# A graph layer on one core: in the first part of group 0, VectorE normalises the tile two batches ahead behind conv1's additions in place of ahead of them

## The chip, the core and the metric

The kernel runs on one core of one Trainium2 chip. The metric is the device time of one execution in microseconds (us); lower is better. A core has five engines that run beside each other, each with a queue of its own: TensorE (PE in the profile; PEld is its loading of weights), VectorE (DVE), ScalarE (ACT), GpSimd (POOL) and SyncE (SP), which here only issues DMAs. Matmuls write to PSUM, of which the kernel uses eight banks; VectorE and ScalarE carry the results from there to SBUF, and so make a bank free for the next matmul.

## What is computed

There are 32 batches of 512 tokens with 256 channels. For each batch (shortened from the reference; the batch norms are constants here and so scale and shift):

```
h   = relu(layernorm(x))                              # over the channels
c   = relu(bn1(conv1(h)))                             # a 256x256 matrix for each token
c   = relu(bn2(conv2(c)) + h)                         # 17 taps along the tokens
s   = h @ w_se.T + b_se                               # three numbers for each token
A   = exp(-|s_n - s_m|^2) * adj
nmp = A @ relu(h @ w_msg.T + b_msg)
r, z, n from a GRU cell with input [c, nmp], state h
out = x + (1 - z) * n + z * h
```

All of it is in 32-bit floats. Conv2 is done by windows of 64 tokens and a transform along the tokens: conv1's result is transformed (`windows_to_freq`), multiplied there with the transformed taps, and transformed back later. The transform of the 17 taps themselves (`weights_to_freq`) is done in the kernel as well, in pieces that are strewn in between the batches of the part that this change touches.

## The kernel before

The 32 batches form two groups of 16 (`GB`). For each group a first part makes h, conv1 and the transform, and a second part (`nodes`) makes the products with the taps and the messages; at the end the gates run over pairs of batches. The change is in the first part of group 0, the branch `if g == 0` in `first_part`. That whole part is built under a manual schedule: every engine carries out its instructions in the order in which the code writes them.

One iteration of the loop for batch b from 2 on writes, in this order:

1. `load_x(b + 3)`: a DMA for the tile of x three batches ahead, on SyncE's queue for b under 3 and on GpSimd's from then on. There are three buffers for x.
2. `statistics(b + 2)`: VectorE's four `bn_stats` (line 392), four `bn_aggr` (394) and one addition (397), then a power on GpSimd that makes rstd (398). These are the means and the factors of the layer norm, two batches ahead.
3. `transpose_h(b + 1)`: TensorE transposes the normalised tile xn (line 419) in eight pieces into two banks, and VectorE takes the relu out of them into hT (423). HT is then written to memory (424) for later parts.
4. `slot()`: for b over 2, a piece of the taps' transform: four matmuls into four banks (line 363; each has two records), and four copies into wst, on ScalarE (373) or VectorE (371). For b = 2 this piece stands ahead of the statistics.
5. `normalise(b + 2)`: four VectorE instructions (line 411) that make xn of the tile two batches ahead from x, the mean and rstd. There are two buffers for xn.
6. `conv1(b)`: 16 matmuls (line 439) from hT of this batch into two banks, eight to each; for each bank an addition of a row on VectorE (442) and a relu on ScalarE (443). The result is h1.
7. `slot()`: a second piece of the taps' transform. Behind every second batch the load of further taps hangs on it, on GpSimd's queue; the finished wst tiles are written to memory from SyncE's queue (377).
8. `windows_to_freq(b - 1)`: the transform of the conv1 result of the batch before: 16 matmuls in two passes of eight records each (line 454) into four banks, and four ScalarE copies into xf (457).
9. `slot()`: a third piece, for b = 12 and b = 14 alone.

All banks come from one pool of eight and are handed out in turn. A plain iteration takes 16 of them (two for the transposes, four for a piece of the taps, two for conv1, four for a piece, four for the windows), so each of these steps finds the same banks in each round, and a step's first matmul waits until the copy or addition that read this bank eight banks ago is done. Conv1 of batch b reads hT that was made one iteration earlier; the transposes of batch b + 1 read xn that was made one iteration earlier.

The order within an iteration of the loop is thus the order in VectorE's queue: statistics, two hT, the copies of the first piece, four normalise, two additions, the copies of the second piece.

Of the kernel before, what the change touches and what calls it, by code (L numbers as in the profile page):

```python
# [162 lines left out]
def gnn_layer(  # L163
# [38 lines left out]
    def bank(name):  # L202
        return psum.tile([P, N], FP, tag="bank", name=name)
# [9 lines left out]
    def load_x(b, queue=nc.sync):  # L213
        X[b] = pools["ahead" if b == GB else "first"].tile([P, NC, D], FP, tag="x", name=f"x_{b}", bufs=1 if b == GB else 3)
        queue.dma_start(X[b], x[b].rearrange("(c p) d -> p c d", p=P))
# [46 lines left out]
    def batch_norm(k, scale, shift, engine):  # L262
        engine.tensor_scalar(scale, at[k + "_v"], BN_EPS, None, op0=ALU.add)
        nc.gpsimd.tensor_tensor(scale, scale, minus_half[:, :DC], op=ALU.pow)
        engine.tensor_mul(scale, scale, at[k + "_g"])
        engine.tensor_mul(shift, at[k + "_m"], scale)
        engine.tensor_sub(shift, at[k + "_b"], shift)
# [11 lines left out]
    def bn1_row(i, v, ones, diags):  # L279
        for c in range(DC):  # L280
            diag = diags[:, i, c, :]
            nc.scalar.activation(diag, ident, AF.Copy, scale=v[:, c : c + 1])
            nc.tensor.matmul(row1[i][:, c * P : (c + 1) * P], ones, diag, start=True, stop=True)
# [6 lines left out]
    def scale_w1():  # L290
        t = W2P.pop("w1")
        for c in range(DC):
            nc.vector.tensor_mul(w1[:, c, :].rearrange("p (i q) -> p i q", i=DC), by_parity(t[:, c, :]),
                                 by_parity(row1[0][:, :D]))
# [93 lines left out]
    def statistics(b):  # L388
        stats = work.tile([P, NC, 6], FP, tag="stats", name=f"stats_{b}")
        mv = work.tile([P, NC, 2], FP, tag="mv", name=f"mv_{b}")  # L390
        for c in range(NC):
            nc.vector.bn_stats(stats[:, c, :], X[b][:, c, :])
        for c in range(NC):
            nc.vector.bn_aggr(mv[:, c, :], stats[:, c, :])
        rstd = work.tile([P, NC], FP, tag="rstd", name=f"rstd_{b}")
        STATS[b] = mv, rstd
        nc.vector.tensor_scalar(rstd, mv[:, :, 1], LN_EPS, None, op0=ALU.add)
        nc.gpsimd.tensor_tensor(rstd, rstd, minus_half[:, :NC], op=ALU.pow)

    def normalise(b, by_scalar=()):  # L400
        mv, rstd = STATS.pop(b)
        XN[b] = pools["first"].tile([P, NC, D], FP, tag="xn", name=f"xn_{b}", bufs=2)
        if by_scalar:
            shift = work.tile([P, NC], FP, tag="shift", name=f"shift_{b}")
            nc.vector.scalar_tensor_tensor(shift, mv[:, :, 0], -1.0, rstd, op0=ALU.mult, op1=ALU.mult)
        for c in range(NC):
            dst, src = by_half(XN[b][:, c, :]), halves(X[b][:, c, :])
            if c in by_scalar:
                nc.scalar.activation(dst, src, AF.Identity, bias=shift[:, c : c + 1], scale=rstd[:, c : c + 1])
            else:  # L410
                nc.vector.tensor_scalar(dst, src, mv[:, c, 0:1], rstd[:, c : c + 1], op0=ALU.subtract, op1=ALU.mult)
        del X[b]
# [14 lines left out]
    def place_h1(b):  # L427
        H1[b] = pools["first"].tile([P, NC, D], FP, tag=f"h1{b % 2}", name=f"h1_{b}", bufs=1)

    def conv1(b):  # L430
        if b not in H1:
            place_h1(b)
        h = N // D
        for c0 in range(0, NC, h):
            p = bank(f"pc1_{b}_{c0}").rearrange("p (c d) -> p c d", d=D)
            for j in range(h):
                c = c0 + j
                for ic in range(DC):
                    nc.tensor.matmul(p[:, j, :], HT[b][:, ic, c * P : (c + 1) * P], w1[:, ic, :],  # L439
                                     start=(ic == 0), stop=(ic == DC - 1))  # L440
            h1 = H1[b][:, c0 : c0 + h, :]
            nc.vector.tensor_add(h1, p, shift1_row[:, None, :].to_broadcast([P, h, D]))
            nc.scalar.activation(h1, h1, AF.Relu)
        if b % GB < GB - 2:
            del HT[b]
# [721 lines left out]
    def first_part(g, freq, between, left=()):  # L1167


        b0, b1 = g * GB, (g + 1) * GB  # L1170
        for b in range(b0, b0 + 3):
            if b not in X and (g == 0 or b == b0):
                load_x(b)
        if g == 0:
            t = XN[b0] = pools["first"].tile([P, NC, D], FP, tag="xn", name="rows", bufs=2)
            ones, diags = t[:, 0, :P], t[:, 1:3, :].rearrange("p i (c m) -> p i c m", m=P)
            nc.vector.memset(ones, 1.0)

            for _ in range(10):
                nc.tensor.matmul(row1[1][:, :P], ident, fr.rearrange("p g c k -> p (g c k)"), start=True, stop=True)  # L1180
            batch_norm("bn1", scale1, shift1, nc.gpsimd)
            bn1_row(0, scale1, ones, diags)
            bn1_row(1, shift1, ones, diags)
        if b0 not in STATS:
            statistics(b0)
        normalise(b0, range(2, NC) if g == 0 else ())
        if g == 0:
            scale_w1()
            shift_w1()
        left = list(left)  # L1190

        def fill():
            for step in left.pop(0) if left else ():
                step()

        if g > 0:
            place_h1(b0)
            load_x(b0 + 1)
            fill()
            load_x(b0 + 2)  # L1200
        transpose_h(b0)
        statistics(b0 + 1)
        fill()
        normalise(b0 + 1, range(NC) if g > 0 else ())
        if g > 0:
            statistics(b0 + 2)
        fill()
        for b in range(b0, b1):
            if b + 3 < b1:
                load_x(b + 3, nc.sync if b < 3 else nc.gpsimd)  # L1210
            if b == b0:
                conv1(b)
                one, two = between(0) if g == 0 else ([], [])
                for step in one:
                    step()
                fill()
                if g == 0:
                    transpose_h(b + 1)
                    statistics(b + 2)
                    normalise(b + 2)  # L1220
                else:
                    normalise(b + 2)
                    transpose_h(b + 1)
                fill()
                xf, last_two = freq(g), two
                continue
            if g == 0:

                slots = last_two if b == b0 + 1 else between(b - b0)

                def slot():
                    for step in slots.pop(0) if slots else ():
                        step()

                if b == b0 + 1:
                    between(b - b0)
                    conv1(b)
                    slot()
                if b == b0 + 2:
                    slot()  # L1240
                if b == b1 - 1:
                    by_chunks(b - 1)
                    load_h(b0)
                if b + 2 < b1:
                    statistics(b + 2)
                if b + 1 < b1:
                    transpose_h(b + 1)
                if b > b0 + 2:
                    slot()
                if b + 2 < b1:  # L1250
                    normalise(b + 2)
                if b > b0 + 1:
                    conv1(b)
                    slot()
                if b == b1 - 1:
                    by_chunks(b)
                windows_to_freq(b - 1, xf)
                slot()
                continue
            if b == b1 - 1:  # L1260
                by_chunks(b - 1)
                load_h(b0)
            if b + 2 < b1:
                statistics(b + 2)
            if b + 1 < b1:
                transpose_h(b + 1)
            if b + 2 < b1:
                normalise(b + 2)
            one, two = between(b - b0)
            conv1(b)  # L1270
            for step in one:
                step()
            windows_to_freq(b - 1, xf)
            for step in two:
                step()
        if g > 0:
            by_chunks(b1 - 1)
        windows_to_freq(b1 - 1, xf)
        return xf
# [273 lines left out]
```

## Time and profile before

| | us |
|---|---|
| median of three runs | 1731.29 (1730.93 to 1731.61) |
| the profiled execution | 1731.29 |
| its span, first to last instruction | 1729.5 |
| TensorE busy in the span | 1714.3 |
| VectorE busy in the span | 1299.3 |
| from conv1 of batch 2 to conv1 of batch 15 | 120.35 |
| of these, TensorE busy | 119.77 |
| of these, VectorE busy | 95.62 |

Busy times are the union of what the profile records for an engine. The ends of matmuls are modelled there, so a stretch in which the engine is busy throughout may still hold waits. The profile gives for each instruction its start and, in brackets, how long its engine sat idle before it and which event ended that idle time. The chain of waits follows the work that ended last back to the start: at each step to what released the instruction, or to the one before it on its engine. In the names, L439 is line 439 of the kernel, and out<-in says what the instruction writes and reads.

Over the stretch from batch 2 to batch 15, the longest waits in total are ScalarE's relu for VectorE's addition (43.0 us, 22 times) and GpSimd's power for VectorE's part of rstd (37.7 us, 7 times). VectorE waited 6.9 us for conv1's matmuls (10 times), 4.3 us for tiles of x (4 times) and once 1.8 us for rstd. TensorE's transposes waited for ScalarE's copies twice, 0.6 us in all.

### The profile page before, as it was taken

The page shows a single profiled execution, that of the slowest core. Times are in us where ns is not written, and L with a number is a line of the kernel's source. Part 1 is how long each engine was busy: PE and PEld are TensorE (multiplying, and loading weights), DVE is VectorE, ACT ScalarE, POOL GpSimd, SP SyncE. Part 2 cuts the span into 40 slices and gives each one's busy share as a digit, 9 for nine tenths or more (in the row PEclk, how much of TensorE's full clock was granted, in tenths as well). Part 3 has the DMA queues.
Part 4 walks back from the last instruction along what each step waited for, and adds up shares of the span by engine and source line. Part 5 has one row for each costly group of instructions (what it writes and reads, how often), then busy time and mean ns, then how long its engine had stood idle before and what let it go on. Part 6 is the DMA issues. An engine that isn't in the chain of part 4 may idle for free.

```text
span 1729.5 us, 24317 instructions
## 1 busy us (share of the span) xinstructions
PE 1714.3 (99%) x7920; PEld 1319.8 (76%) x7920; DVE 1299.3 (75%) x2599; ACT 692.1 (40%) x1669; POOL 1086.6 (63%) x1074
## 2 busy tenths in 40 slices
PE   8999999999999999999999999999999999999998
PEld 6777888888998888887877778777877787778744
DVE  7876877776996677676587778877887778777867
ACT  4556655553446555554322232232323232323221
POOL 3331788687655677777767657665667556755551
PEclk9999999999999999999999999999999999999999
DMA  9989987885778888888433454235523553345423
GB/s 250 304 283 263 262 237 242 252 231 183 269 246 232 268 246 238 234 254 309 115 106 71 79 128 119 69 69 128 128 67 70 120 128 91 75 91 128 110 55 73
DMA packets 311681, 295.07 MB, mean 171 GB/s; under 512 B 147436, under 2 KB 241164, under 8 KB 311172
## 3 DMA queue, kind: packets, MB, share of 16 engines
q1 hardware_dynamic: 301588, 265.17, 55.9%
q0 software_dynamic: 6960, 26.65, 4.8%
q10 hardware_dynamic: 3008, 1.72, 0.3%
q8 instruction: 63, 1.03, 0.2%
q14 instruction: 62, 0.51, 0.1%
HBM read 194.31 MB, written 99.16 MB: 170 GB/s over the span
## 4 chain that ended last, share of the span: by engine, by line
PE 93%; DVE 2%; DMA 2%; POOL 1%; SPq 1%; issue 1%; ACT 0%; POOLq 0%; DVEq 0%
PE pg L915 29%; PE pn L932 16%; PE py L503 11%; PE pn L670 10%; PE pm L558 6%; PE pc L439 6%; PE pc L878 3%; PE px L454 3%; PE pd L608 2%; PE pw L363 1%; PE phT L419 1%; PE pz L932 1%; PE pg L932 1%; PE pn L653 1%; PE pc L881 1%
## 5 line engine op out<-in xcount | busy, mean ns | idle before, releaser
L470 POOL TENSOR_TENSOR wsum<-wt 128x512 f32<-128x512 f32 x66 | 93.6, 1418 | 97.9 <-DMA wt<-wd 69.2
L503 PE MATMUL py<-wt,xf 128*128 128x256 f32 x640 | 154.2, 384 | 0.0
L915 PE MATMUL pg<-te,sw 128*128 128x256 f32 x600 | 154.0, 379 | 0.0
L906 ACT ACTIVATE rz<-rz,brz 128x256 f32<-128x256 f32 x180 | 86.3, 504 | 147.1 <-DVE rz L921 147.1
L503 PEld LDWEIGHTS py<-wt,xf 128*128 128x128 f32 x640 | 117.1, 190 | 34.9 <-issue 21.2
L915 PEld LDWEIGHTS pg<-te,sw 128*128 128x128 f32 x600 | 114.0, 190 | 15.5
L618 DVE TENSOR_TENSOR A<-A,at 128x512 f32<-128x512 f32 x124 | 118.5, 995 | 6.3 <-ACT A L614 2.8
L915 PE MATMUL pg<-tn,sw 128*128 128x256 f32 x480 | 123.2, 379 | 0.0
L915 PE MATMUL pg<-hn,sw 128*128 128x256 f32 x480 | 123.2, 379 | 0.0
L932 PE MATMUL pn<-tn,sw_n 128*128 128x512 f32 x256 | 120.3, 592 | 0.0
L1077 ACT ACTIVATE pn<-nt,vech 128x512 f32<-128x512 f32 x45 | 31.1, 692 | 219.1 <-DVE nt L1074 139.8
L439 PE MATMUL pc<-w,hT 128*128 128x256 f32 x512 | 117.7, 383 | 0.9 <-DVE hT L423 0.9
L558 PE MATMUL pm<-wmsg,hq 128*128 128x259 f32 x512 | 117.3, 381 | 0.0
L439 PEld LDWEIGHTS pc<-w,hT 128*128 128x128 f32 x512 | 94.6, 190 | 23.9 <-issue 6.4
L812 POOL TENSOR_TENSOR tn<-hn 128x512 f32<-128x512 f32 x64 | 86.2, 1367 | 35.6 <-PE pn L932 35.6
L558 PEld LDWEIGHTS pm<-wmsg,hq 128*128 128x128 f32 x512 | 96.5, 189 | 14.6
L915 PEld LDWEIGHTS pg<-hn,sw 128*128 128x128 f32 x480 | 91.1, 190 | 18.3 <-issue 3.4
L915 PEld LDWEIGHTS pg<-tn,sw 128*128 128x128 f32 x480 | 91.2, 190 | 12.4
L921 DVE TENSOR_TENSOR ct<-pg,ct 128x256 f32<-128x256 f32 x180 | 74.6, 415 | 33.0 <-PE pg L915 23.5
L932 PEld LDWEIGHTS pn<-tn,sw_n 128*128 128x128 f32 x256 | 48.6, 190 | 61.2 <-issue 50.9
L932 PE MATMUL pn<-hn,sw_n 128*128 128x512 f32 x192 | 90.5, 593 | 0.1
L915 PE MATMUL pg<-tec,sw 128*128 128x256 f32 x300 | 89.2, 379 | 0.0
(236 smaller groups left out, 4321.3 us busy)
## 6 DMA issues: line engine op xcount, KB each, us to landing
wt<-wd SPq DMA_DIRECT2D x80, 512.0 KB, 6.2
adj<-in_adj_dram SPq DMA_DIRECT2D x128, 256.0 KB, 5.8
wd<-wst SPq DMA_DIRECT2D x64, 320.0 KB, 5.4
yd<-y SPq DMA_DIRECT2D x76, 256.0 KB, 5.1
hd<-hT SPq DMA_DIRECT2D x32, 512.0 KB, 4.7
nd<-nmp SPq DMA_DIRECT2D x32, 512.0 KB, 3.0
xb<-in_x_dram SPq DMA_DIRECT2D x128, 128.0 KB, 6.3
out_dram<-xb SPq DMA_DIRECT2D x122, 128.0 KB, 2.8
```

The lines of the kernel that those rows point to most:

```text
L439: nc.tensor.matmul(p[:, j, :], HT[b][:, ic, c * P : (c + 1) * P], w1[:, ic, :], start=(ic == 0), stop=(ic == DC - 1))
L454: nc.tensor.matmul(p[:, j * 2 * L : (j + 1) * 2 * L], H1[b][:, c0 + j, ic * P : (ic + 1) * P], fwd, start=True, stop=True)
L470: nc.gpsimd.tensor_tensor(t, WT[g, u][:, 0], WT[g, u][:, 1], op=ALU.add)
L503: nc.tensor.matmul(dst, v[:, ic, :], w[:, ic, :], start=(ic == 0), stop=(ic == DC - 1))
L558: nc.tensor.matmul(p[:, : D + NS], hq[:, ic, c * P : (c + 1) * P], wmsg[:, ic, :], start=(ic == 0), stop=(ic == DC - 1))
L618: nc.vector.tensor_mul(A[b][:, mc, :], EXP.pop((b, mc)), AT.pop((b, mc)))
L670: nc.tensor.matmul(bk, left[:, k, :], right[:, k, :], start=(first and k == 0), stop=(k == 1), skip_group_check=True)
L812: nc.gpsimd.tensor_tensor(dst[:, k], x[:, k], y[:, k], op=op)
L906: nc.scalar.activation(at(dst), at(src), AF.Sigmoid, bias=brz[:, o : o + 1], scale=sign)
L915: nc.tensor.matmul(bk, SW["hk"][:, k, s, :], c if k == 2 else hn[:, k], start=(onto is None and k == 0), stop=(k == K3 - 1), skip_group_ch ...
L921: nc.vector.tensor_tensor(at(dst), at(x), at(y), op=op)
L932: nc.tensor.matmul(bk[:, t], weight(q, k, o), terms[k][q][:, t], start=(first and i == 0), stop=(i == len(ks) - 1), skip_group_check=True)
```

## The change

`normalise(b + 2)` is written behind `conv1(b)` instead of ahead of it. The conditions stay the same. It holds for b from 2 to 13; for b = 1, conv1 stands further up and nothing changes, and from b = 14 on there is no tile two batches ahead in this group.

```diff
                 if b > b0 + 2:
                     slot()
+                if b > b0 + 1:
+                    conv1(b)
                 if b + 2 < b1:
                     normalise(b + 2)
                 if b > b0 + 1:
-                    conv1(b)
                     slot()
```

Conv1's matmuls and relus are on TensorE and ScalarE, where the normalise has no instruction, so the order on these two engines is as before, and so is that of GpSimd and of the DMA queues. On VectorE the order becomes: statistics, two hT, the copies of the first piece, two additions, four normalise, the copies of the second piece.

## The prediction

> **What bounds the kernel now.** I read the page first, then the chain of waits in order of time over the first 220 us, then the timeline of the stage that the change touches, then the DMA share in windows of 2 us. From the page:
>
> ```profile
> PE 93%; DVE 2%; DMA 2%; POOL 1%; SPq 1%; issue 1%; ACT 0%; POOLq 0%; DVEq 0%
> ```
>
> TensorE carries the chain; VectorE holds 2% of it. So VectorE's order matters only where TensorE is kept waiting. TensorE's busy share cannot show where that is (10.00 of 10 us in most windows), since waits inside a stream of matmuls count as busy. I therefore took the pace of the loop: the times at which conv1's matmuls of batch b start (line 439). They are 27.57 for batch 2, then 37.47, 46.43, 55.39, 64.34, 74.63, 83.58, 92.54, 101.50, 110.93, 119.88, 130.02 (batch 13), 138.97, 147.92. The plain distance is 8.95 us. Longer ones are 2 to 3 (9.90), 6 to 7 (10.29), 10 to 11 (9.43), and 12 to 13 (10.14, of which 1.03 is a third piece of the kernel transform; 0.16 remains). The loss is 0.95 + 1.34 + 0.48 = 2.77 us. The plain iteration, of batch 4, in the timeline (start, duration, engine, idle time before it):
>
> ```profile
> 46.43 3.72 PE L439 MATMUL pc<-w,hT 128*128 128x256 f32 x16
> 47.77 1.37 DVE L411 TENSOR_SCALAR xn<-x,mv,rstd 128x256 f32<-128x256 f32 x4
> 49.05 0.68 DVE L442 TENSOR_TENSOR h<-pc,shift_row 128x512 f32<-128x512 f32 x1
> 50.08 1.10 PE L363 MATMUL pw<-w2p,taps 17*80 17x512 f32 x8
> 50.19 0.69 DVE L442 TENSOR_TENSOR h<-pc,shift_row 128x512 f32<-128x512 f32 x1 [0.46 <-PE pc L439]
> 51.11 2.44 PE L454 MATMUL px<-fwd,h 128*128 128x160 f32 x16
> 51.33 0.69 DVE L371 COPY wst<-pw 80x512 f32<-80x512 f32 x1 [0.45 <-PE pw L363]
> 53.39 1.04 PE L419 MATMUL phT<-ident,xn 128*128 128x128 f32 x8
> 54.03 1.29 DVE L423 TENSOR_SCALAR hT<-phT 128x512 f32<-128x512 f32 x2 [0.22 <-PE phT L419]
> 55.39 3.72 PE L439 MATMUL pc<-w,hT 128*128 128x256 f32 x16
> ```
>
> Here VectorE waits for TensorE three times and TensorE for nobody: TensorE sets the pace. Two of the three losses, in the chain of waits (start, duration, what):
>
> ```profile
> 31.41 1.05 DVE xn L411 x3
> 32.46 0.61 DVE h L442
> 33.09 1.23 ACT h L443 x2
> 34.32 0.48 ACT wst L373
> ...
> 34.85 1.14 PE phT L419 x8
> ...
> 67.24 0.97 POOL rstd L398
> 68.24 1.38 DVE xn L411 x4
> 69.62 0.61 DVE h L442
> 70.25 0.62 ACT h L443
> ...
> 71.38 0.57 ACT wst L373
> 72.00 1.14 PE phT L419 x8
> ```
>
> Both run the same way: normalise (xn), then conv1's addition (h), ScalarE's relu, ScalarE's copies out of the kernel-transform banks (wst), and only then may TensorE reuse these banks. The normalise stands at the head. In batch 6 it was itself held 1.77 us by GpSimd's rstd, which was late behind a load of vectors.
>
> **What the Trainium skill says.** "PSUM — Partial Sum Buffer", section "Engine vs sequencer instructions", has VectorE's and ScalarE's queues strictly first in, first out. The trace agrees: the additions of batch 6 started at 69.53, though their matmuls had ended by 67.99. "Perfetto Trace Analysis", "Optimizing Scalar/DVE Operations", says that part of a recorded duration overlaps the next instruction. It does: a normalise instruction is recorded at 402 ns, but four take 1.28 us from the first to the next addition. I count from start to start. The same page, "Identifying the Most-Contended Engine", calls matmul busy share a poor measure; the 10.29 us distance inside fully busy windows shows it.
>
> **The change part by part.** Nothing is added or removed: 12 times (batches 2 to 13) four VectorE instructions step behind two. TensorE, ScalarE, GpSimd and the DMA queues keep their order, and no queue is passed.
>
> Plain iteration, times from C, the start of conv1's matmuls:
> - Eight of the 16 matmuls fill the first bank by about C+1.94 (half of 3.65, and 0.11 from matmul to addition as at 50.08 and 50.19), the rest by C+3.76. VectorE is through with its transform copies at about C+1.4. Before, the normalise filled the time up to C+2.62. Now the first addition runs at C+1.94, 0.68 earlier, VectorE idles some 1.1 us, and the second runs at C+3.76 as before.
> - The normalise follows at C+4.4 and ends at C+5.7. The transposes that read it start at C+6.83 (53.26 for their weight load): 1.1 us to spare. Cost: nothing, hidden by the transform piece and the DFT matmuls.
> - What stood behind the second addition is late by what is left of 1.28 us. The transform copy starts at 52.1 in place of 51.33 (0.8). Statistics follow 0.6 later, hT 1.79 after those (28.02 to 29.81 in batch 2): 54.5 in place of 54.03. The next copies end near C'+1.7, before the next first addition can start at C'+1.94, so the lateness is swallowed each round. The banks concerned are wanted later: the copy's ends 52.8, wanted 54.6; those of hT end 55.8, wanted 59.04. VectorE's own work from addition to addition is 7.5 us (0.65 + 1.28 + 0.6 + 1.79 + 1.29 + 1.25 + 0.65), under 8.95. Sum: 0.
>
> The three late iterations:
> - Batch 2. VectorE comes from the start-up with no slack (9.9 of 10 us busy). Both banks were full by 31.2, but the additions started at 32.38. Now they start at 31.08, when hT is done. ScalarE's relus and copies come 1.3 us earlier: the bank that the transposes wanted is free at 33.5, before the DFT matmuls end at 34.4. The normalise ends at 33.65, also in time. Conv1 of batch 3 starts near 36.45: 0.95 to 1.0 gained.
> - Batch 6. The additions no longer wait for rstd (68.2): they run at 66.5 and 68.1, the normalise at 68.8 to 70.1, the transposes want it at 71.2. All of the 1.34 goes.
> - Batch 10. An x tile landed 2.22 us late, the normalise ran at 104.55 and the additions at 105.83, though the second bank was full at 105.2. They now lead: 0.48 goes.
>
> Sum: 0.95 + 1.34 + 0.48 = 2.77. It carries on if what follows is started by TensorE's progress and not by a DMA backlog. The DMA share is near 1.0 for long stretches, but falls to 0.51 and 0.59 at 50 to 54, 0.64 and 0.59 at 68 to 72, 0.36 at 88, 0.09 at 106, 0.10 at 124 and 0.04 at 146 to 148: the backlog empties about every second batch, so loads come earlier too. The next stage waits for an adjacency tile (166.8) that is queued behind this stage's last weight stores, which follow its last matmuls; I let it move along.
>
> The profiled execution took 1731.29 us around a span of 1729.5, equal to the median. I take 2.7 off: **1728.6 us**, 0.16%, just under the 0.2% that a measurement of this kernel can tell from no change.
>
> **Rivals.**
> - *The gain is lost to transfers.* TensorE running 1 to 2.8 us ahead finds x tiles no earlier: statistics, which stand ahead of hT and the additions, hold VectorE. For: four waits for x in the stage, 4.3 us in all, and the saturated DMA from 34 to 50. Against: the dips. It can take back what was won and no more, as a held VectorE is back on the old schedule: gain 0 to 2, say 1730.4.
> - *Faster by over 0.2%.* The gain also takes along the 0.16 of batch 12 and the stall at the next stage's head, where eight exponent matmuls spread from 171.17 to 173.79 in place of 1.07 us (1.5 lost). 2.77 + 0.16 + half of 1.5 = 3.7: 1727.6. Against: that stall hangs on the adjacency load, which shifts with the rest.
> - *Slower.* TensorE's transposes begin to wait for the normalise, now the last thing before them. The margin is 1.1 us; it decides from C+6.83. Were the normalise 0.6 us later than this in each of 12 rounds, 7.2 us less the 2.8 won: 1735.7. For: it now stands behind the second bank. Against: its start is fixed by the matmuls at C+4.4 and it lasts 1.28.
> - *It does nothing*: excluded as such, the order does change; in time it is the end of the first rival.
>
> **How the numbers follow.** Forecast 0.60, lost to transfers 0.22, faster 0.10, slower 0.08. Within 0.2% are the first two, 0.82. The range goes from 1727.2 (3.4 gained, and the 0.7 by which runs differ) to 1732.0 (nothing gained, and the same 0.7); what it leaves out is most of the slower case.
>
> **What would show it.** In the changed profile: distances of 8.95 for 2 to 3, 6 to 7 and 10 to 11; first additions near C+1.94 with about 1.1 us of idle VectorE before the second; no wait of the transposes (line 419) for xn; the adjacency tile read 2.7 us earlier than at 166.81. Transposes waiting for xn in most rounds, or an adjacency load that lands no earlier, would prove it wrong.

## The result and the profile after

| | before | changed |
|---|---|---|
| median of 20 runs | 1731.12 us (1729.38 to 1733.39) | 1728.24 us (1725.36 to 1737.42) |
| ratio, 95% interval | | 0.9981 (0.9974 to 0.9988) |
| span of the profiled execution | 1729.5 us | 1725.1 us |
| from conv1 of batch 2 to conv1 of batch 15 | 120.35 us | 117.73 us |

The changed kernel is faster by 2.9 us, a fifth of a percent. Of the 4.4 us between the two spans, 2.62 lie in the loop that was changed (120.35 less 117.73) and 0.55 ahead of it: conv1 of batch 2 started at 27.02 in place of 27.57. The code is the same up to there, and in the runs below that start lies between 26.87 and 27.75, so these 0.55 are the spread of single runs. The remaining 1.2 lie behind the loop, where single runs differ by more than that: from the first adjacency tile to the end they take 1561.3 to 1563.8 us.

The page of the changed kernel has this line for the chain of waits, by engine:

```profile
PE 96%; DVE 1%; POOL 1%; issue 1%; DMA 0%; SPq 0%; ACT 0%; ACTq 0%; POOLq 0%; DVEq 0%
```

TensorE's share of the chain went from 93% to 96%; what VectorE, DMA and the DMA queue held before has mostly gone. A plain iteration, that of batch 5, in the timeline of the changed kernel:

```profile
53.79 3.72 PE L439 MATMUL pc<-w,hT 128*128 128x256 f32 x16
55.82 0.69 DVE L442 TENSOR_TENSOR h<-pc,shift_row 128x512 f32<-128x512 f32 x1 [0.47 <-PE pc L439]
57.44 1.10 PE L363 MATMUL pw<-w2p,taps 17*80 17x512 f32 x8
57.55 0.69 DVE L442 TENSOR_TENSOR h<-pc,shift_row 128x512 f32<-128x512 f32 x1 [1.03 <-PE pc L439]
58.16 1.37 DVE L411 TENSOR_SCALAR xn<-x,mv,rstd 128x256 f32<-128x256 f32 x4
58.47 2.44 PE L454 MATMUL px<-fwd,h 128*128 128x160 f32 x16
59.45 0.68 DVE L371 COPY wst<-pw 80x512 f32<-80x512 f32 x1
60.75 1.04 PE L419 MATMUL phT<-ident,xn 128*128 128x128 f32 x8
62.75 3.72 PE L439 MATMUL pc<-w,hT 128*128 128x256 f32 x16
```

With C for the start of conv1's matmuls, the first addition stands at C+2.03, VectorE idles 1.03 us, the second addition is at C+3.76 as before, the normalise ends at C+5.74, and the next conv1 starts 8.96 us after this one, as before. The plain iteration is neither faster nor slower.

The two late iterations shown of before, and that of batch 10, in the chain of waits of the changed kernel in order of time:

```profile
27.19 3.46 PE pc L439 x16
30.64 1.03 PE pw L363 x8
31.67 2.37 PE px L454 x16
34.04 0.87 PE phT L419 x8
34.92 1.03 PE pw L363 x8
35.95 3.65 PE pc L439 x16
...
66.47 1.03 PE pw L363 x8
67.50 2.37 PE px L454 x16
69.87 0.87 PE phT L419 x8
...
105.70 0.87 PE phT L419 x8
106.57 1.25 PE pw L363 x8
107.82 3.65 PE pc L439 x16
```

In batches 2 and 6, where VectorE and ScalarE, and in batch 6 GpSimd and a DMA too, stood in the chain before, TensorE now stands alone. In batch 10 it stood alone before too; there the loss showed as a longer piece of the kernel transform (1.50 us at 109.49 before, where 1.03 is usual). That piece, now at 106.57, is still longer by 0.22.

### The profile page after: what moved, and what is told of

The parts are those of the page before. It is cut to its first block, busy times and chain, and to the rows that moved or that the text cites. A ratio compares the mean times of both kernels' runs of the same rounds, so it can differ in the third digit from the quotient of the medians.

```text
span 1725.1 us, 24328 instructions
## 1 busy us (share of the span) xinstructions
PE 1711.9 (99%) x7920; PEld 1319.5 (76%) x7920; DVE 1299.3 (75%) x2599; ACT 691.7 (40%) x1669; POOL 1086.9 (63%) x1074
## 3 DMA queue, kind: packets, MB, share of 16 engines
q8 instruction: 63, 1.03, 0.3%
## 4 chain that ended last, share of the span: by engine, by line
PE 96%; DVE 1%; POOL 1%; issue 1%; DMA 0%; SPq 0%; ACT 0%; ACTq 0%; POOLq 0%; DVEq 0%
PE pg L915 29%; PE pn L932 16%; PE py L503 11%; PE pn L670 10%; PE pm L558 6%; PE pc L439 6%; PE px L454 4%; PE pc L878 3%; PE pd L608 2%; PE pw L363 2%; PE phT L419 1%; PE pz L932 1%; PE pg L932 1%; PE pn L653 1%; PE pc L881 1%
```

## The experiments

All runs change group 0's first part alone. The loop is read from one profile each: the distances between conv1's starts, and the stretch from batch 2 to batch 15. That stretch shows a tenth of a microsecond, where the time of a whole run moves by a few; but it is that of one execution, and where a transfer lands late it need not be the same in the next. A plain distance is 8.96 (10.14 from 12 to 13, with its third piece, and 8.86 from 2 to 3); the table has what departs from this. `e5_behind_stats`, where nearly all depart, comes at the end.

```
kernel            2-3   4-5   6-7   7-8   8-9  10-11 12-13  stretch  ratio to before (95%)
before            9.90  8.96 10.28  8.96  8.96  9.43 10.14  120.35
changed           8.86  8.96  8.96  8.96  8.96  9.18 10.14  117.73  0.9981 (0.9974 to 0.9988)
e1_three          8.86 10.47  8.96  8.96 10.03  8.96 10.87  120.82  0.9996 (0.9988 to 1.0004)
e2_nine           9.91  8.96 10.61  8.96  8.96  9.59 10.14  120.85  1.0004 (0.9996 to 1.0012)
e3_vectors        9.91  8.96  8.96  9.99  8.96 10.02 10.14  120.65  1.0000 (0.9991 to 1.0008)
e4_behind_copy    8.86  9.69  8.96  8.96  8.96  8.96 11.05  119.42  0.9987 (0.9980 to 0.9993)
e7_early_x        9.91  8.96 10.31  8.96  8.96  8.96 10.14  119.92  0.9994 (0.9986 to 1.0002)
e8_both           8.86  8.96  8.96  8.96  8.96  8.96 10.14  117.50  0.9979 (0.9970 to 0.9987)
e9_x_vectors      9.91  8.96  8.96  9.79  8.96  8.96 10.14  119.39  0.9988 (0.9981 to 0.9994)
e10_vectors_last  9.91  8.96  8.96  8.96  9.19  8.96 10.14  118.79  0.9997 (0.9988 to 1.0005)
e11_x_vectors_last 9.91 8.96  8.96  8.96  8.96  8.96 10.14  118.56  0.9980 (0.9972 to 0.9988)
e12_three_x       8.86  8.96  9.32  9.22  8.96  8.96 10.14  118.14  0.9979 (0.9971 to 0.9987)
```

### Which of the moved batches count

Two complements: in `e1_three` the new order holds for `b in (2, 6, 10)`, the three late iterations; in `e2_nine` for `b not in (2, 6, 10)`.

```diff
-                if b > b0 + 1:
+                late = b in (2, 6, 10)
+                if b > b0 + 1 and late:
                     conv1(b)
                 if b + 2 < b1:
                     normalise(b + 2)
                 if b > b0 + 1:
+                    if not late:
+                        conv1(b)
                     slot()
```

> The move is kept for batches 2, 6 and 10 alone; the other nine batches have the old order. Theory A (the gain lies in the three late iterations, each by itself): distances of conv1's starts 2 to 3, 6 to 7 and 10 to 11 as in the changed kernel (8.86, 8.96, about 9.2), all others 8.96; conv1 of batch 2 to conv1 of batch 15 is 117.7 us as in the changed kernel (120.35 before), time 2.6 below before. Rival B (every batch moved gives its share through earlier relus): a quarter of it, about 119.7 us, time 0.7 below before. Rival C (the gain lies outside the loop, at the start or in the next part): the loop is near 117.7 but the time stays away from the changed kernel's.

> The complement: the move for the nine batches other than 2, 6 and 10, which keep the old order. Theory A: 2 to 3, 6 to 7 and 10 to 11 stay long (9.9, about 10.3, 9.4), all others 8.96, so that the stretch from batch 2 to batch 15 is 120.2 to 120.4 us and the time is that of before within 0.5 us. Rival B: three quarters of the gain, about 118.4 us and 2 us less time. Rival C: no long distance tells anything, time as in the changed kernel.

The nine alone bring nothing, as theory A says: 120.85. But the three alone bring nothing either. Their own distances became short as expected (8.86, 8.96, 8.96), and new long ones came up at 4 to 5, 8 to 9 and 12 to 13. So the gain is not a sum over three places, which refutes theory A, and it is not a share for each batch, which refutes rival B. The times say the same: theory A wants a ratio of 0.9985 for the three, rival B 0.9988 for the nine, and neither lies in its interval. Batch 4 of `e1_three`, in its timeline:

```profile
44.57 1.41 DVE L392 BATCH_NORM_STATS2 stats<-x 128x6 f32<-128x256 f32 x4 [3.26 <-DMA x<-in_x_dram]
44.68 3.72 PE L439 MATMUL pc<-w,hT 128*128 128x256 f32 x16
...
48.78 1.37 DVE L411 TENSOR_SCALAR xn<-x,mv,rstd 128x256 f32<-128x256 f32 x4
...
50.06 1.28 DVE L442 TENSOR_TENSOR h<-pc,shift_row 128x512 f32<-128x512 f32 x2
50.78 1.23 ACT L443 ACTIVATE h<-h 128x512 f32<-128x512 f32 x2 [4.94 <-DVE h L442]
...
51.91 1.53 ACT L373 COPY wst<-pw 80x512 f32<-80x512 f32 x3
...
52.53 1.14 PE L419 MATMUL phT<-ident,xn 128*128 128x128 f32 x8 [0.32 <-ACT wst L373]
```

VectorE waited 3.26 us for a tile of x. Behind it in VectorE's queue stands the whole iteration: statistics, hT, copies, normalise, additions; then ScalarE's relu and copies, then TensorE. It is the same chain as in the late iterations of before, with another head: there the start-up and a late rstd, here a late tile. The tile is that of an even batch, which is loaded from GpSimd's queue behind the load of further taps. Two things met: TensorE was 1.75 us earlier than before (44.68 for 46.43; 0.70 of this by its start), and the tile came 1.1 us later (44.57 for 43.46). Why it came later isn't shown; in the changed kernel, the same up to here but for batch 3's order, it came at 43.75. How much the three lose is thus in part this execution's own.

### The same head elsewhere: how late may x be?

How far the statistics start from the start of conv1 in the same iteration (negative: ahead of it), and what the following distance lost against 8.96 (10.14 from 12 to 13). Shown are those nearest to the point from which it costs, and those past it; where rstd was late too, the batch is left out. In `e4_behind_copy`, told further down, the additions stand where the change puts them.

```
order where it happened   kernel, batch          statistics less conv1      lost
old                       e10_vectors_last, 6     62.20 -  63.92 = -1.72    0
old                       e10_vectors_last, 8     80.45 -  81.84 = -1.39    0.23
old                       e1_three, 12           117.73 - 118.93 = -1.20    0.73
old                       before, 10             100.35 - 101.50 = -1.15    0.47
old                       e2_nine, 10            101.02 - 102.01 = -0.99    0.63
old                       e3_vectors, 10          99.98 - 100.54 = -0.56    1.06
old                       e1_three, 8             81.48 -  82.03 = -0.55    1.07
old                       e1_three, 4             44.57 -  44.68 = -0.11    1.51
new                       changed, 8              79.56 -  80.66 = -1.10    0
new                       changed, 4              43.75 -  44.84 = -1.09    0
new                       changed, 6              61.79 -  62.75 = -0.96    0
new                       e4_behind_copy, 10      99.04 -  99.77 = -0.73    0
new                       changed, 10             98.47 -  98.58 = -0.11    0.22
new                       e4_behind_copy, 12     117.96 - 117.68 = +0.28    0.91
new                       e4_behind_copy, 4       45.69 -  45.30 = +0.39    0.73
```

In batches 3 to 11 of the old order the loss is the lateness beyond C-1.62, to within 0.01: 1.62 - 1.39 = 0.23, 1.62 - 0.55 = 1.07, 1.62 - 0.11 = 1.51. In the new order two points lie above zero, and both put the bound at C-0.33 (0.33 - 0.11 = 0.22, 0.33 + 0.39 = 0.72). The difference, 1.29 us, is what four normalise instructions take from start to start. Batch 12 with its third piece has other bounds, C-1.93 and C-0.63 by its two points, and the same difference. Batches 2 and 13, whose pieces of the taps stand or are shared out otherwise, don't follow these numbers: before, batch 13 lost nothing at C-0.72. The change moves the point in time by which VectorE must be there by just the work that no longer stands ahead of the additions.

### The late rstd of batch 6

`e3_vectors` keeps the old order and moves GpSimd's work on the loaded vectors, which had held rstd in batch 6, one batch later; `e10_vectors_last` moves it to batch 14, behind the last power.

```diff
         load_vectors,
+        lambda: None,
         vectors,
```

```diff
         load_vectors,
-        vectors,
-        scale_embedding,
+        *[lambda: None] * 2,
         partial(nc.sync.dma_start, back, nc.inline_tensor(back_np, name="dft_back").ap()),
+        *[lambda: None] * 5,
+        vectors,
+        scale_embedding,
```

> The old order throughout, but GpSimd's work on the loaded vectors (and the two steps after it in the list) comes one batch later, so that the power for rstd of batch 8 is not queued behind it. Theory A: the normalise of batch 8 is not held, 6 to 7 falls from 10.28 to 8.96 without the change, 2 to 3 (9.9) and 10 to 11 (9.4) stay; the stretch is 119.0 us, time 1.3 below before. If instead the distance 6 to 7 were long because of VectorE's order by itself, it stays at 10.3 and the time stays too. A loss that merely moves to 7 to 8 would show there.

The distance 6 to 7 became 8.96, and 7 to 8 became 9.99. The timeline of `e3_vectors` says why:

```profile
71.68 0.81 POOL L215 DMA_DIRECT2D x<-in_x_dram  x1
72.48 0.51 POOL L255 COPY vech<-vec 64x28 f32<-64x28 f32 x2
...
75.06 1.01 POOL L399 TENSOR_TENSOR rstd<-rstd,minus_half 128x4 f32<-128x4 f32 x1
...
76.11 1.51 DVE L412 TENSOR_SCALAR xn<-x,mv,rstd 128x256 f32<-128x256 f32 x4 [2.00 <-POOL rstd L399]
```

The vectors had long landed, but the small operations on them run for 2.6 us (72.48 to 75.06) behind a load of taps, and now held the rstd of the next batch. So this run moved the cause and didn't remove it. The move to the end does.

> The old order and the old loads of x, but GpSimd's work on the vectors goes to the last batches, behind the last power for rstd, so that it can hold none. Theory A (three separate causes): 6 to 7 falls to 8.96, nothing else changes, stretch 119.0 us. Theory A2 (a late x tile and the long chain behind it in VectorE's queue are the limit; TensorE can't get ahead of the transfers): 6 to 7 falls to 8.96, and the 1.3 us come back at 8 to 9 or 10 to 11, where the wait of the statistics for x grows; stretch 119.8 to 120.5.

118.79: theory A's number. 6 to 7 is 8.96, 7 to 8 too, and only 0.23 came back at 8 to 9. TensorE could keep 1.3 us of advance here, against the strict form of theory A2. In this execution the late rstd thus cost its own 1.3 us in the old order. It was the fastest of 13, though (1727.69, median 1730.92), and in time the run is not to be told from before; whether other executions lose the 1.3 us again to late tiles, as theory A2 has it, stays open.

### The late tile of x

`e7_early_x` keeps the old order and loads each tile one batch earlier from batch 2 on; three buffers are enough, as the normalise of tile b + 1 stands one iteration back. `e8_both` has the change with it, `e12_three_x` the new order for batches 2, 6 and 10 with it, `e9_x_vectors` and `e11_x_vectors_last` the old order, it, and the vectors moved as in `e3_vectors` and `e10_vectors_last`.

```diff
-            if b + 3 < b1:
-                load_x(b + 3, nc.sync if b < 3 else nc.gpsimd)
+            for n in (b + 3,) if g > 0 or b < 2 else (b + 3, b + 4) if b == 2 else (b + 4,):
+                if n < b1:
+                    load_x(n, nc.sync if b < 3 else nc.gpsimd)
```

> The old order throughout, but from batch 2 on each tile of x is loaded one batch earlier (into the buffer that the batch before has just left), so that the tiles of the even batches are no longer queued behind the load of further taps. Theory A2 (one recurring cause: a late x tile, through statistics, hT, copies, normalise and additions in VectorE's queue, holds TensorE's banks; the change only shortens this chain by the 1.28 us of the normalise): VectorE no longer waits for x, 10 to 11 falls from 9.43 to 8.96, and no loss appears at 4 to 5 or 8 to 9. 2 to 3 (9.9, start-up) and 6 to 7 (rstd behind the vectors, about 10.3) stay. Stretch about 119.9 us, time 0.5 below before. Theory A (three separate causes): the same 0.5. Rival D (transfers as a whole are the limit, so an earlier x pushes something else back): a loss appears elsewhere and the stretch stays at 120.3 or more.

> The old order, x tiles one batch earlier as in the run before, and GpSimd's work on the vectors one batch later. Theory A2: with x in time the gain at 6 to 7 is no longer paid back at 7 to 8 and 10 to 11: only 2 to 3 stays long (9.9), the stretch is 118.6 us, time 1.8 below before, without the change in order. Rival D: the stretch stays near 120.3 as with the vectors alone (120.65).

> The changed kernel with x tiles one batch earlier. Theory A2: the last long distance (10 to 11, 9.18) falls to 8.96 and VectorE's waits for x go (7.6 us in the changed kernel), the stretch is 117.5 us; in time 0.2 below the changed kernel, which is not to be told from it in so many runs. Rival D: stretch above 117.7.

> The old order with both taken away: x tiles one batch earlier, and the work on the vectors behind the last power. Theory A2: only 2 to 3 (start-up, 9.9) stays long, stretch 118.6 us, time about 1.7 to 2 below before. If the order on VectorE had a price of its own in plain batches, more would stay.

> The move for batches 2, 6 and 10 alone, with x tiles one batch earlier. Theory A2: the losses at 4 to 5, 8 to 9 and 12 to 13 that this choice of batches showed without the earlier x (10.47, 10.03, 10.87) go, all distances are 8.96 (12 to 13: 10.14), stretch 117.5 us, time as with the changed kernel and earlier x. If those losses came from the mixed order itself and not from x, they stay and the stretch is above 119.

`e7_early_x` is 119.92, as expected: VectorE waits for no x, 10 to 11 is 8.96, and what stays is the start-up and the late rstd. `e9_x_vectors` missed its 118.6 for the reason seen in `e3_vectors` (9.79 from 7 to 8, rstd late by 1.9 us). `e11_x_vectors_last`, with both heads taken away, is at 118.56 in the old order, with 2 to 3 alone still long. It is also as fast as the changed kernel: 0.9980 of before. Its loop accounts for 1.8 us of that; the time fell by 3.4 (2.1 to 4.8), and where the rest lies isn't shown. `e8_both` is at 117.50, where all distances are short; in time (0.9979) it can't be told from the changed kernel. `e12_three_x` shows that the losses of `e1_three` at 4, 8 and 12 came from x: with x in time they are gone, though VectorE once waited 1.6 us for rstd, behind the additions of batch 6 (new order). What stands behind it came late, the additions of batch 7 (old order) among it, and the distances 6 to 7 and 7 to 8 lost 0.36 and 0.26, so that it missed its 117.5. Rival D, that earlier loads only push other transfers back, falls with `e7_early_x` and `e8_both`.

### How far back may the normalise go?

`e4_behind_copy` puts it behind the copy of the second piece; `e5_behind_stats` behind the statistics of the next tile.

```diff
                 if b > b0 + 1:
                     conv1(b)
+                    slot()
                 if b + 2 < b1:
                     normalise(b + 2)
-                if b > b0 + 1:
-                    slot()
```

```diff
                 if b + 2 < b1:
                     statistics(b + 2)
+                if b0 + 2 < b < b1 - 1:
+                    normalise(b + 1)
                 if b + 1 < b1:
                     transpose_h(b + 1)
                 if b > b0 + 2:
                     slot()
+                if b == b0 + 1:
+                    normalise(b + 2)
                 if b > b0 + 1:
                     conv1(b)
-                if b + 2 < b1:
-                    normalise(b + 2)
-                if b > b0 + 1:
                     slot()
```

> The normalise goes one place further back than in the changed kernel, behind the copy of the second piece of the taps' transform too: its end moves from about 5.7 to about 6.3 us after conv1's start, while the transposes want it at 6.83. Theory A with its margin of 1.1 us: nothing lost, the stretch from batch 2 to batch 15 is 117.5 to 117.9 us and no distance grows, transposes don't wait for xn. Rival (the margin is used up already, so that every later step costs): up to 0.6 us for each of 12 batches, stretch about 124.9 us, time 4 above before.

> The normalise of a tile goes behind the statistics of the next one, so that it ends some 8.1 us after conv1's start, 1.3 us past the point at which the transposes want it. If the margin in a plain iteration is what the prediction says (1.1 us), TensorE's transposes now wait for xn in each of 12 batches, each distance grows from 8.96 to 9.7 to 10.0, the stretch is 126 to 130 us, time 6 to 10 above before. If VectorE's place for the normalise didn't matter, the stretch would stay below 120.

`e4_behind_copy` loses nothing in plain iterations: ten of its thirteen distances are as short as can be. Twice a tile of x landed after conv1's start (45.69 against 45.30 in batch 4, 117.96 against 117.68 in batch 12), which cost 0.73 and 0.91, and 0.27 more from 13 to 14, where the transposes waited for xn. So 119.42 in place of 117.7: the plain margin holds and the expectation, which had left late tiles out, missed. Why its tile 6 landed later than in the changed kernel (43.75) can't be told from one run.

`e5_behind_stats` is 1.0147 (1.0131 to 1.0163, four runs) of before, stretch 149.83: past the margin the loss is real and much larger than the 126 to 130 expected. TensorE's waits up to 200 us in its list of waits (who waits, for what; us in total, times, longest):

```profile
PE phT L419 <- DVE xn L411: 10.4, 10, 3.6
PE phT L419 <- ACT xf L457: 4.3, 6, 0.7
```

And three windows of 5 us of the same kernel: length, then busy time and count of TensorE, its weight loads, VectorE, ScalarE and GpSimd; the last three figures are the granted clock, the DMA share and GB/s.

```profile
40.00:45.00 5.00, 5.00 (x17) 3.87 (x14) 1.98 (x3) 1.27 (x3) 0.00 (x0) 0.56 0.95 360
50.00:55.00 5.00, 4.89 (x27) 3.21 (x28) 3.76 (x8) 1.17 (x3) 0.97 (x1) 1.00 0.87 263
...
155.00:160.00 5.00, 5.00 (x18) 2.73 (x19) 2.07 (x3) 1.55 (x3) 0.00 (x0) 0.50 0.41 151
```

TensorE's transposes, which waited for nothing in this loop in the changed kernel, wait in each iteration from 3 to 13 (of the ten waits for xn one, 0.2 us, lies ahead of the loop, and four are for later pieces). The six waits put down to ScalarE's xf fit xn as well: there, as in the waits for xn, the transposes start 0.55 to 0.56 us after the first normalise instruction (in iteration 3 alone it is 0.77). Where the clock is 1.00 the distance is 10.63 (52.71 to 63.34), a loss of 1.67 in place of 0.7 to 1.0: the statistics ahead of the normalise started at C+5.5 (58.22), not at C+5.0, because the copy before them still waits for its matmuls, and the normalise ended at C+8.8. The longest distances, 12.73, 12.46 and 16.92 us (2 to 3, 3 to 4 and 12 to 13), lie around the two longest falls of the clock: 0.75 from 35 to 40 us and 0.56 in the first window, and 0.50 in the last.

## Why the prediction was right, and where not

It said 1728.6, within 0.2% of before, and 1728.24 came, with a ratio whose interval lies below 1. Two places of the timelines, batch 6 of the changed kernel, and batch 10 before and then changed:

```profile
65.99 1.27 DVE L442 TENSOR_TENSOR h<-pc,shift_row 128x512 f32<-128x512 f32 x2
66.13 1.01 POOL L398 TENSOR_TENSOR rstd<-rstd,minus_half 128x4 f32<-128x4 f32 x1
```

```profile
100.35 1.41 DVE L392 BATCH_NORM_STATS2 stats<-x 128x6 f32<-128x256 f32 x4 [2.22 <-DMA x<-in_x_dram]
101.50 3.72 PE L439 MATMUL pc<-w,hT 128*128 128x256 f32 x16
...
98.47 1.41 DVE L392 BATCH_NORM_STATS2 stats<-x 128x6 f32<-128x256 f32 x4 [2.51 <-DMA x<-in_x_dram]
98.58 3.72 PE L439 MATMUL pc<-w,hT 128*128 128x256 f32 x16
```

Step by step:

- **Plain iteration at no cost: right.** First addition at C+2.03 (1.94 predicted), 1.03 us idle (1.1), normalise to C+5.74 (5.7), the copy at C+5.66 (5.67), transposes at C+6.83 without a wait for xn. That nothing in plain iterations pays is shown by `e2_nine`.
- **Batch 2, 0.95 to 1.0: right**, 1.04 (9.90 to 8.86), in every kernel with the new order there.
- **Batch 6, all of 1.34: right in size and cause.** The additions started at 65.99, before rstd was there (66.13 to 67.14). A late tile held the first of them to C+3.24 (C+2.16 was forecast), at no cost. `e10_vectors_last` shows the price of the late rstd by itself, 1.3 us in its one profile. The prediction put the 10.29 us inside fully busy windows; TensorE is busy for 9.97 of them. Its point stands, as 0.32 us of visible idle time are much less than the 1.33 lost.
- **Batch 10, 0.48: the term that was mis-sized.** 0.25 came (9.43 to 9.18). The step assumed that x keeps its place relative to TensorE, since "the backlog empties about every second batch, so loads come earlier too". It didn't: the statistics of batch 10 started 1.15 us ahead of conv1 before and 0.11 ahead after, and those of batch 4 started at 43.75 in place of 43.46 although TensorE was 1.6 us earlier. VectorE's waits for x grew from 4.3 to 7.6 us. The new order still bore x at C-0.33; x came 0.22 later than that.
- **The sum of three places, each by itself: wrong as a picture**, though the total fitted (2.62 for 2.77). `e1_three` has the three places and no gain. The first rival, the gain lost to transfers, was the true danger: TensorE ahead of its old schedule meets late tiles in batches 4, 8 and 12. What averts it is that these batches have the new order too and so bear x 1.29 us later: in the changed kernel's profile batches 4 and 8 came 0.5 us too late for the old order and lost nothing. The prediction counted nine of twelve moves as idle; `e1_three` shows that they are not. That the total came out near 2.77 all the same was in this part luck.
- **The gain carries on: right.** The first adjacency tile is turned at 162.90 in place of 166.81, 3.9 us earlier for the 2.7 forecast; 0.55 of this is the earlier start, 2.62 the loop, and 0.7 lies between loop and tile, a stretch that takes 17.7 to 19.2 us in these runs. The eight exponent matmuls behind it, which before were spread from 171.17 to 173.79, took 2.07 us in the chain. The 0.16 of batch 12, which the rival of a larger gain took for a loss, stayed: the distance with the third piece is 10.14 wherever nothing is late.
- **The slower rival** needs the normalise to end past C+6.83; `e5_behind_stats` went there and is 1.5% slower. Its place was right. At a clock of 1.00 its price, 0.6 for 0.6, was on the high side (1.67 lost for 2.0 us past the point); what it left out is that TensorE's waits were followed by a lower clock.

Left open: by how much the landing of one and the same tile of x differs from run to run, and whether TensorE's advance itself delays it by earlier weight stores ahead in the DMA queues. It fits tile 6 (43.25 to 43.46 in three runs with the old order in batch 2, 43.75 to 45.69 in three with the new one), but was not tried.

## What to carry to other kernels

In a queue that runs in order, put the work that frees a buffer of the bounding engine ahead of work that is wanted only an iteration later, even if a gap opens in front of it; in plain iterations this cost nothing here, and where inputs were late it moved the deadline by the work's full length, 1.29 us. Don't add up stalls seen at different places as if each could be removed alone: here the engine that got ahead met the next late transfer, so give the whole loop the longer deadline, or the transfer an earlier start. And measure such a change by the loop's own distances in the profile, where a tenth of a microsecond shows, when the whole time tells two tenths of a percent at best. Where late transfers decide, one execution is not enough for that.

## What was not expected of the hardware

Behind four of TensorE's waits in `e5_behind_stats`, of 1.86, 1.68, 1.44 and 3.60 us (they ended at 36.40, 93.45, 137.95 and 153.95), its granted clock, 1.00 throughout this stretch in the changed kernel, fell: to 0.56, 0.66, 0.67 and 0.50 in the windows of 5 us from 40, 95, 140 and 155 us. The Trainium skill, "TensorE: Matmul & The Clock Gate", "What's actually happening", says that the clock halves after an idle window of about 3.4 us. Three of these four waits are much shorter than that, so here the measurement differs from the page. Nor did every such wait lower the clock: in the kernel before, one of 1.76 us at the start-up (it ended at 8.18) left it at 1.00, as did the waits of 0.7 to 0.9 us in each round of `e5_behind_stats` from 50 to 90 us. What else decides isn't shown by these runs.
